# A nucleus search's branch in a graph kernel: two small tie arms for a five-armed switch, its neighbours moved, and the output stores on another queue

## The chip, the cores and the metric

The kernel runs on one core of a Trainium2 chip. The metric is device microseconds of one execution. PE is TensorE, DVE is VectorE, ACT is ScalarE, POOL is GpSimd and SP is SyncE, which here only issues DMAs.

## What is computed

N = 2708 nodes, 512 features. A graph attention layer with 8 heads comes first; its output X goes through two diffusion steps and a layer norm. Cut to what matters:

```python
feats = einsum('nf,hfd->hnd', X, W); dense = leaky_relu(e_self + e_neigh) + mask
X = relu(softmax(dense) @ feats + b)                     # attention over adj
Rf, Rb = S / rowsum(S), S / colsum(S)[:, None]           # S = adj + I
Xf = Xb = Xa = X; Z = 0
for s in range(2):
    logits = (Xa @ W1) @ W2 @ (Xa @ W3).T                # 2708 x 2708
    idx = argsort(-logits)                               # ties: the lower index first
    k_i = sum(cumsum(softmax(sorted logits)) < 0.9) + 1  # the nucleus of each row
    A = softmax(where(rank < k_i, logits, -inf))
    Xf, Xb, Xa = Rf @ Xf, Rb @ Xb, A @ Xa
    Z = Z + Xf @ U1[s] + Xb @ U2[s] + Xa @ U3[s]
out = layernorm(x + Z) * gamma + beta                    # in outline
```

The costly question is the nucleus: for each row, the smallest set of largest probabilities that holds 0.9 of the mass.

## The kernel before

The rows are cut into 22 tiles of 128 (the last has 20) and these into 11 pairs; pair g is tiles 2g and 2g+1. A pair's work in a diffusion step passes through these stages:

- `products`: PE makes a 128 x 2708 tile of logits (L534) and ACT copies it into `p` (L536).
- `exp`: DVE takes the row maxima `nmx` (L561), ACT exponentiates (root and full, L569 to L573) with the row sums.
- `points`: POOL guesses three thresholds for each row from the row sums by a fitted power (L578 to L588): `x` and `pts`, their fourth powers `th`, the negative `nth`, and `thr`, `top`, `cap`.
- the looks: ACT (L566) sums signs of p + nth, and POOL (L591 to L593) makes of that the mass above each guess, in `pts`.
- `Opened`: `ready` (L641 to L643, L655) and `bracket` (L661 to L676), small DVE operations, put those masses into an interval for each row.
- `search`: ROUNDS = (2, 4) rounds in step 0 and 1. Each picks a point in the interval and measures the mass above it in each tile (L647, one pass of a tile).
- `finish`: the entries of the interval are cut out (`kept_from` L773, or `kept_ranked` L778 to L781 in step 1, where equal values are told apart by rank), the largest 8 or 16 are sorted out by MAX8 (L849, L851), and the cut and the denominator `den` follow.
- `branch`: flags of all rows are folded into one integer `code_i`. 0: nothing is left to do. 1, 2, 3: a tile of the pair, or both, has ties at the cut that rank does not settle. 4: a row fell short of its cut. DVE loads it into a register and switches (L936) over five arms. Arm 4 holds more rounds, a second finish with a switch of its own, and in that a third.
- `rden` (L958) is the reciprocal of `den`. `keep`, the pair's kept probabilities, goes to `attended`: PE transposes it (L1107), ACT copies the transposes into `at` (L1111), PE multiplies by Xa (L1127).

The engines' orders in a diffusion step are the order of emission for PE, ACT, DVE and SP (a manual schedule); POOL's order is the scheduler's. The loop over g runs the search of pair g+1 on DVE beside the attended stage of pair g on PE. Between its rounds the search calls `early` (puts `exp` of pair g+2 in: `nmx` on DVE, and a list `fills` for ACT) and what it returns: `norms`, the layer norm's ends of the pair before (L1190, L1191; step 1 only), and `pending`, which splits results for DRAM. In the last two pairs nothing follows to be filled in.

`attended` is a generator. Between its groups n of transposes and products it issues `fills` and `others`. The latter are steps of `part`: the products of S with Xf and Xb (PE L1021, L1024) and with U (L1042), whose operands `hl` and `s_r` are loaded by SP (L1014, L1016) and `u_k` by SP (L1040); then `xe` on ACT and `z` on POOL (L1065, L1067). In step 1 ACT scales the product into `yo` (L1135), POOL adds z (L1137), and `normed` follows: moments (L137 to L140), a load of the input row (`xw`, SP, L1187), the two DVE operations of `rest`, and a store of the finished rows, issued by POOL (L1192).

Step 1 has one piece of work more at its start: `counted` (L1226, DVE), the ranks that settle ties. It comes in two halves, 22 operations in all; the second half stands after the first pair's `nmx` and covers ACT's and POOL's first work on that pair.

The branch as it was:

```python
            opened = None
            if go == 0 and then:
                opened = then()               # Opened(next pair): ready, before the switch
            what = nc.values_load(code_i[0:1, 0:1], engines=[DVE], min_val=0, max_val=1 << G, ...)
            for arm in tc.Switch({DVE: what}, (1 << G) + 1):
                if 0 < arm < 1 << G:
                    ties([x for x in tiles if arm >> x[0] & 1])
                elif arm == 1 << G and go == 0:
                    rounds(MORE_ROUNDS); choose(); finish(1)
                elif arm == 1 << G and go == 1:
                    ...
                    finish(2)
                elif arm == 1 << G:
                    bisect()
                if opened:
                    opened.bracket()
```

Of the kernel before, what the change touches and what calls it, by code (L numbers as in the profile page):

```python
# [15 lines left out]
OP = mybir.AluOpType  # L16
# [17 lines left out]
BISECT_STEPS = 28  # L34
# [11 lines left out]
MORE_ROUNDS = 3  # L46
# [7 lines left out]
def kernel(  # L54
# [428 lines left out]
    for s in range(STEPS):  # L483
        for i in range(2):
            nc.vector.memset(powers[:, s, i], GUESS[s][i])
    about = const.tile([P, STEPS, len(ABOUT), G], F32, name="about")
    for s in range(STEPS):
        for j, m in enumerate(ABOUT):
            nc.vector.memset(about[:, s, j], m * math.exp(GUESS[s][2]))
# [15 lines left out]
    class Logits:  # L505
# [33 lines left out]
        def exp(self, looks=True):  # L539
# [19 lines left out]
            for i, t in enumerate(self.grp):  # L559
                pr = rows[t]  # L560
                nc.vector.tensor_reduce(nmx[:pr, 0, i:i + 1], self.p[i][:pr], axis=AX.X, op=OP.max, negate=True)  # L561

# [13 lines left out]
            def points():  # L576
                x0 = small.tile([P, 2, G], F32, name="x0")
                gp.tensor_tensor(x0, self.sums, powers[:, self.s], op=OP.pow)  # L578
                gp.tensor_tensor(x0[:, 0], x0[:, 0], x0[:, 1], op=OP.mult)
                x = self.pts[:, :, 0]  # L580
                gp.tensor_tensor(x, x0[:, 0].unsqueeze(1).to_broadcast([P, NA, G]), about[:, self.s], op=OP.mult)
                gp.tensor_scalar(x, x, X_LO * 1.2, 0.9995, op0=OP.max, op1=OP.min)
                gp.tensor_tensor(self.th, x, x, op=OP.mult)
                gp.tensor_tensor(self.th, self.th, self.th, op=OP.mult)
                gp.tensor_scalar(self.nth, self.th, -1.0, None, op0=OP.mult)  # L585
                gp.tensor_scalar(self.thr, self.tot, P_NUC, None, op0=OP.mult)
                gp.tensor_scalar(self.top, self.tot, 1.0 + CURVE, None, op0=OP.mult)
                gp.tensor_scalar(self.cap, self.tot, CAP, None, op0=OP.mult)  # L588
# [22 lines left out]
    class Opened:  # L611
# [4 lines left out]
        def __init__(self, lg, looked, junk):  # L616
            _, small, _ = lg.pools
            self.lg, self.looked = lg, looked
# [59 lines left out]
    def search(lg, o, junk, early, late, then=None):  # L678
# [14 lines left out]
        tiles, aim, mass = o.tiles, o.aim, o.mass  # L693
# [7 lines left out]
        def rounds(n, aim_at=None):  # L701
            for it in range(n):
                v.tensor_tensor(d, ends[:, 1, 0:2], ends[:, 0, 0:2], op=OP.subtract)
                v.tensor_scalar(d[:, 1], d[:, 1], -1e-12, None, op0=OP.min)
                v.reciprocal(fr, d[:, 1])
                v.tensor_mul(fr, fr, ends[:, 0, 1])
                v.tensor_scalar(fr, fr, -0.95, -0.05, op0=OP.max, op1=OP.min)
                v.tensor_mul(fr, fr, d[:, 0])
                v.tensor_tensor(cur[:, 0], ends[:, 0, 0], fr, op=OP.subtract)
                v.tensor_mul(th, cur[:, 0], cur[:, 0])  # L710
                v.tensor_mul(th, th, th)
                if it in (aim_at or ()):
                    v.tensor_copy(fr, g0)
                    aim(g0, th)
                    v.tensor_tensor(fr, fr, g0, op=OP.subtract)
                    v.tensor_tensor(ends[:, :, 1], ends[:, :, 1], fr.unsqueeze(1).to_broadcast([P, 2, G]), op=OP.add)
                if begun:
                    begun.pop()()
                for i, pr in tiles:
                    mass(i, pr, th[:pr, i:i + 1], cur[:pr, 2, i:i + 1])  # L720
                v.tensor_tensor(fr, lg.top, cur[:, 2], op=OP.subtract)
                v.reciprocal(fr, fr)
                v.tensor_tensor(cur[:, 1], fr, g0, op=OP.subtract)
                v.scalar_tensor_tensor(side, cur[:, 1].unsqueeze(1).to_broadcast([P, 2, G]), 0.0, sides,
                                       op0=OP.is_ge, op1=OP.not_equal)
                v.copy_predicated(ends, side.unsqueeze(2).to_broadcast([P, 2, 3, G]),
                                  cur.unsqueeze(1).to_broadcast([P, 2, 3, G]))
                if it == s and aim_at is not None:
                    begun.append(early())

        begun = []
        rounds(ROUNDS[s], (0,) if s else ())
        for rest in begun:
            rest()
# [5 lines left out]
        def choose():  # L740


            v.tensor_tensor(low, ends[:, 0, 2], thr, op=OP.is_lt)
            v.tensor_copy(kept[:, 0], ends[:, 1, 0])
            v.tensor_copy(kept[:, 1], ends[:, 1, 2])
            v.copy_predicated(kept[:, 0], low, ends[:, 0, 0])
            v.copy_predicated(kept[:, 1], low, ends[:, 0, 2])
            v.tensor_mul(th, kept[:, 0], kept[:, 0])
            v.tensor_mul(th, th, th)

        choose()
# [32 lines left out]
        def ties(of):  # L784


            if lg.rank is not None:
                for x in of:
                    kept_from(*x)
# [3 lines left out]
            for i, pr in of:  # L793
                v.tensor_scalar(junk_b[:pr], ps_[i][:pr], cut[:pr, i:i + 1], None, op0=OP.is_equal)
# [8 lines left out]
        def bisect():  # L803
# [3 lines left out]
            v.memset(ends[:, 0, 0], X_LO)  # L807
            v.memset(ends[:, 1, 0], X_HI)
            for _ in range(BISECT_STEPS):
                v.tensor_add(cur[:, 0], ends[:, 0, 0], ends[:, 1, 0])  # L810
                v.tensor_scalar(cur[:, 0], cur[:, 0], 0.5, None, op0=OP.mult)
                v.tensor_mul(th, cur[:, 0], cur[:, 0])
                v.tensor_mul(th, th, th)
                for i, pr in tiles:
                    v.scalar_tensor_tensor(junk_b[:pr], ps_[i][:pr], th[:pr, i:i + 1], ps_[i][:pr],
                                           op0=OP.is_ge, op1=OP.mult, accum_out=cur[:pr, 2, i:i + 1])
                v.tensor_tensor(side[:, 0], cur[:, 2], thr, op=OP.is_ge)
                v.tensor_tensor(side[:, 1], cur[:, 2], thr, op=OP.is_lt)
                v.copy_predicated(ends[:, 0, 0], side[:, 0], cur[:, 0])
                v.copy_predicated(ends[:, 1, 0], side[:, 1], cur[:, 0])  # L820
            v.tensor_mul(d, ends[:, :, 0], ends[:, :, 0])
            v.tensor_mul(d, d, d)
            half = junk.shape[1]
            for i, pr in tiles:
                v.scalar_tensor_tensor(keep[i][:pr], ps_[i][:pr], d[:pr, 1, i:i + 1], ps_[i][:pr],
                                       op0=OP.is_ge, op1=OP.mult, accum_out=over[:pr, i:i + 1])
                v.scalar_tensor_tensor(ps_[i][:pr], ps_[i][:pr], d[:pr, 0, i:i + 1], ps_[i][:pr],
# [13 lines left out]
        def finish(go):  # L841
# [16 lines left out]
            if lg.rank is not None:  # L858
# [28 lines left out]
                return branch(go)  # L887
# [25 lines left out]
            branch(go)  # L913

        def branch(go):
# [15 lines left out]
            opened = None  # L931
            if go == 0 and then:
                opened = then()
            what = nc.values_load(code_i[0:1, 0:1], engines=[DVE], min_val=0, max_val=1 << G,
                                  skip_runtime_bounds_check_because="at most 1 << G")
            for arm in tc.Switch({DVE: what}, (1 << G) + 1):  # L936
                if 0 < arm < 1 << G:
                    ties([x for x in tiles if arm >> x[0] & 1])
                elif arm == 1 << G and go == 0:
                    rounds(MORE_ROUNDS)  # L940
                    choose()
                    finish(1)
                elif arm == 1 << G and go == 1:
                    v.copy_predicated(th, short, vn[:, :, nx - 1])
                    v.copy_predicated(kept[:, 1], short, den)
                    finish(2)
                elif arm == 1 << G:
                    bisect()
                if opened:
                    opened.bracket()  # L950
            if go == 0:
                nxt.append(opened)

        nxt = []
        late()
        finish(0)
        rden = small.tile([P, G], F32, name="rden1")
        v.reciprocal(rden, den)  # L958
        return (keep, rden), nxt[0]
# [5 lines left out]
    for s in range(STEPS):  # L965
        last = s == STEPS - 1
        with ExitStack() as st:
# [121 lines left out]
            spread_z = {}  # L1089

# [5 lines left out]
            def attended(grp, keep, rden, fills, others, first=3):  # L1096
# [20 lines left out]
                for n, (i, t, cs) in enumerate(steps):  # L1117
                    pr = rows[t]
                    nxt = turned(*steps[n + 1]) if n + 1 < len(steps) else None
                    if n:  # L1120
                        paced(left, 1)
                    if n >= first:
                        paced(fills, 1 + i if last else 1 if n > 8 else 2)
# [58 lines left out]
            def normed(t, y):  # L1182
# [6 lines left out]
                def rest():  # L1189
                    nc.vector.scalar_tensor_tensor(y[:pr], y[:pr], mean, g_b[:pr], op0=OP.subtract, op1=OP.mult)  # L1190
                    nc.vector.scalar_tensor_tensor(y[:pr], y[:pr], rs, xb[:pr], op0=OP.mult, op1=OP.add)  # L1191
                    nc.gpsimd.dma_start(out=out[cols[t], :], in_=y[:pr])  # L1192
# [53 lines left out]
            with tc.manual_schedule(engines={PE, ACT, DVE, SP}):  # L1246
# [8 lines left out]
                for step in steps:  # L1255
                    step()
# [7 lines left out]
                ready = opened = None  # L1264
                looks, left = [], []
                for g in range(-1, NP):
# [23 lines left out]
                    def early(g=g):  # L1290
                        if g + 2 < NP:
                            fills.extend(lg[g + 2].exp())
                        return lambda: [rest() for rest in norms] + [paced(pending, len(pending))]
# [30 lines left out]
                    if g + 1 < NP:  # L1324
                        if g == 0:
                            opened = Opened(lg[1], True, junk)
                            opened.bracket()
                        then = (lambda g=g: Opened(lg[g + 2], True, junk)) if 0 <= g < NP - 2 else None
                        ready, opened = search(lg[g + 1], opened, junk, early, late, then)
# [5 lines left out]
                if last:  # L1335
                    for rest in [normed(t, y) for t, y in done]:
                        rest()

# [30 lines left out]
```

## Time and profile before

| | us |
|---|---|
| runs | 3674.58, 3666.84, 3673.27 (median 3673.27) |
| profiled execution | 3675.58, span 3673.8 |
| attention layer | to about 1087 |
| diffusion step 0 | about 1087 to 2235 |
| diffusion step 1 | about 2300 to 3668 |
| busy: ACT, POOL | 1499.2 (41%), 867.6 (24%) |

In the profile the idle time of an engine stands with what ended it. "issue" means that the engine waited for nothing that the profile shows. Lines are those of the kernel. The granted clock is that of PE, 1.00 being full speed. Two searches took a tie arm, both in step 1 with one tile each.

### The profile page before, as it was taken

What the parts mean: (1) busy time and instruction counts of PE and PEld (TensorE: products, weight loads), DVE (VectorE), ACT (ScalarE), POOL (GpSimd) and SP (SyncE); (2) the same over time, 40 slices, a digit from 0 to 9 for tenths busy, and PEclk for the clock granted to TensorE, in tenths of its full rate; (3) what the DMA queues carried; (4) which work ended last, traced back from release to release, by engine and by line L of the source; (5) the groups of instructions that cost most, each with busy time, mean ns of one, the idle gap of its engine ahead of it and who ended that gap; (6) DMA issues with size and microseconds to landing.
All of it is one profiled execution on the core that took longest, in us unless ns stands there. A gap on an engine that the chain in (4) does not pass through costs nothing. (4 is left out here: it accounts for less than half of the span.)

```text
span 3673.8 us, 34163 instructions
## 1 busy us (share of the span) xinstructions
PE 3339.6 (91%) x10791; PEld 1725.2 (47%) x10791; DVE 2668.4 (73%) x4832; ACT 1499.2 (41%) x2248; POOL 867.6 (24%) x1072
## 2 busy tenths in 40 slices
PE   8998999998967889999999999978899799999977
PEld 4433333333444454645555454544555455555543
DVE  4587888989965565546563652796889888888984
ACT  2343212011113656666565641235445545456600
POOL 4114241514321021111121111321213232122211
PEclk9999999999979999999999999989999899999989
DMA  4477424232227343526344442782465255654443
GB/s 117 149 250 249 141 76 157 75 106 100 85 80 268 134 165 126 206 87 212 107 162 167 139 168 75 268 282 96 157 215 201 103 181 198 226 198 167 162 133 130
DMA packets 247979, 580.17 MB, mean 158 GB/s; under 512 B 33306, under 2 KB 67050, under 8 KB 243492
## 3 DMA queue, kind: packets, MB, share of 16 engines
q1 hardware_dynamic: 226695, 503.59, 41.0%
q0 software_dynamic: 21040, 73.88, 5.2%
q8 instruction: 86, 1.41, 0.2%
q14 instruction: 158, 1.29, 0.1%
HBM read 471.68 MB, written 105.68 MB: 157 GB/s over the span
## 5 line engine op out<-in xcount | busy, mean ns | idle before, releaser
L1127 PE MATMUL a<-va,at 128*128 128x512 f32 (+2 forms) x1936 | 900.7, 605 | 55.3 <-ACT at L1111 55.1
L442 PE MATMUL po<-e,fw 128*65 128x512 f32 (+4 forms) x2112 | 840.2, 553 | 36.2 <-DVE e L440 20.9
L440 DVE SCALAR_TENSOR_TENSOR e<-r_b,kk,a_c 128x512 f32<-128x512 f32 (+4 forms) x1056 | 751.6, 741 | 74.8 <-PE po L442 25.8
L566 ACT ACTIVATE junk_a<-p,nth 128x2708 uint8<-128x2708 f32 (+1 forms) x240 | 612.7, 2553 | 102.3 <-POOL nth L585 98.1
L1021 PE MATMUL q<-hl,s_r 128*128 128x512 f32 x1936 | 525.2, 420 | 57.5 <-DMA s_r<-s_d 57.3
L1127 PEld LDWEIGHTS a<-va,at 128*128 128x128 f32 (+2 forms) x1936 | 341.6, 189 | 433.6 <-issue 346.1
L442 PEld LDWEIGHTS po<-e,fw 128*65 128x65 f32 (+1 forms) x2112 | 286.7, 140 | 549.4 <-issue 271.9
L1021 PEld LDWEIGHTS q<-hl,s_r 128*128 128x128 f32 x1936 | 362.0, 191 | 208.2 <-issue 58.9
L647 DVE SCALAR_TENSOR_TENSOR junk<-p,th 128x2708 bf16<-128x2708 f32 (+1 forms) x132 | 411.5, 3118 | 3.8
L1042 PE MATMUL q<-u_k,tt 128*128 128x512 f32 x704 | 321.2, 599 | 10.6 <-DMA u_k<-in_L_gnn_U_dram 10.6
L1111 ACT COPY at<-t 128x512 f32<-128x512 f32 (+3 forms) x308 | 140.0, 476 | 466.8 <-PE t L1107 466.1
L1024 PE MATMUL q<-s_r,hl 128*128 128x512 f32 (+1 forms) x1056 | 281.3, 411 | 11.1 <-DMA s_r<-s_d 11.1
L536 ACT COPY p<-t 128x452 f32<-128x452 f32 (+2 forms) x264 | 130.2, 537 | 371.5 <-PE t L534 303.8
L1024 PEld LDWEIGHTS q<-s_r,hl 128*128 128x128 f32 x1056 | 188.1, 189 | 98.2 <-issue 51.3
L534 PE MATMUL t<-keys,q_t 128*128 128x452 f32 x528 | 155.7, 420 | 73.0 <-ACT p L536 59.3
L1042 PEld LDWEIGHTS q<-u_k,tt 128*128 128x128 f32 x704 | 135.6, 193 | 162.7 <-issue 158.6
L851 DVE MAX8 vn<-keep 128x8 f32<-128x2708 f32 (+1 forms) x66 | 196.8, 2981 | 2.3
L424 ACT ACTIVATE s_c<-a_c 128x512 fp32r<-128x512 f32 (+3 forms) x132 | 76.2, 577 | 247.7 <-DMA a_c<-in_adj_t_dram 119.0
L1167 PE MATMUL a<-u_k,v_t 128*128 128x512 f32 (+1 forms) x352 | 173.4, 629 | 0.8 <-DMA u_k<-in_L_gnn_U_dram 0.8
L1107 PEld LDWEIGHTS t<-ident,keep 128*128 128x128 f32 (+1 forms) x968 | 114.6, 140 | 111.1 <-issue 83.8
L561 DVE TENSOR_REDUCE nmx<-p 128x1 f32<-128x2708 f32 (+1 forms) x44 | 129.3, 2966 | 48.8 <-ACT p L536 48.8
L1107 PE MATMUL t<-ident,keep 128*128 128x128 f32 (+1 forms) x968 | 147.5, 275 | 18.6 <-DVE ends L662 10.7
(305 smaller groups left out, 3339.3 us busy)
## 6 DMA issues: line engine op xcount, KB each, us to landing
s_r<-s_d SPq DMA_DIRECT2D x330, 256.0 KB
hl<-vhl_d SPq DMA_DIRECT2D x132, 512.0 KB
hl<-fhl_d SPq DMA_DIRECT2D x132, 512.0 KB
hl<-bhl_d SPq DMA_DIRECT2D x132, 512.0 KB
u_k<-in_L_gnn_U_dram SPq DMA_DIRECT2D x184, 256.0 KB
arow<-in_adj_dram SPq DMA_DIRECT2D x21, 1354.0 KB
s_d<-s_c SPq DMA_DIRECT2D x88, 256.0 KB
a_c<-in_adj_t_dram SPq DMA_DIRECT2D x84, 256.0 KB
```

The costliest lines, as they stand in the source:

```text
L440: nc.vector.scalar_tensor_tensor(e[:pr, :cw], r_b[:pr, i, :cw], kk[:pr, t, hd:hd + 1], a_c[t][:pr, :cw], op0=OP.max, op1=OP.mult)
L442: nc.tensor.matmul(po[i][:, :cw], lhsT=fw[:pr, t, hd, :], rhs=e[:pr, :cw], start=(t == 0), stop=(t == NT - 1))
L534: nc.tensor.matmul(pl[:, :c1 - c0], lhsT=q[:, i], rhs=self.keys[:, c0:c1], start=(i == 0), stop=(i == 1))
L566: nc.scalar.activation(junk[:pr], self.p[i][:pr], func, **kw)
L647: nc.vector.scalar_tensor_tensor(self.junk_b[:pr], p, th, p, op0=OP.is_ge, op1=OP.mult, accum_out=dst)
L851: v.max(vs, keep[0][:pr])
L1021: nc.tensor.matmul(half[j], lhsT=s_r[:, j * P:(j + 1) * P], rhs=hl[:, h], start=(c == 0 and h == 0), stop=(c == NT - 1 and h == 1))
L1024: nc.tensor.matmul(half[j][:, :w], lhsT=hl[:, h, j * P:(j + 1) * P], rhs=s_r[:, :w], start=(c == 0 and h == 0), stop=(c == NT - 1 and h == 1))
L1042: nc.tensor.matmul(half[j], lhsT=across_t[-1][:, k, j * P:(j + 1) * P], rhs=u_k, start=(start and k == 0), stop=(start and k == KD - 1))
L1107: nc.tensor.transpose(pt[:rows[c], j, :pr], keep[i][:pr, cols[c]], ident[:pr, :pr])
L1127: nc.tensor.matmul(pa[:pr], lhsT=at[:rows[c], j, :pr], rhs=va[:rows[c], c, :], start=(c == 0), stop=(c == NT - 1))
L1167: nc.tensor.matmul(pz[i][:rows[t]], lhsT=v_t[i][:, k, :rows[t]], rhs=u_k, start=(k == 0), stop=(k == KD - 1))
```

## The change

- The switch becomes nested conditions: if the code is not 0, then bisection for 4, else one arm for each tile. The arms with more rounds and a second finish are gone, and `bisect` is written anew: 27 geometric steps from 2^-16 in place of 28 arithmetic ones.
- `ready` and `bracket` of the next pair no longer stand before and in the branch, but just before the next search, behind `rden` and the moments of `normed`.
- `points` makes `nth` at once (the fit's powers times four), then `th`, then `pts` by a fourth root (a pow on POOL). `nth` is POOL's 7th operation of the pair instead of the 10th.
- The two maxima `nmx` leave `exp`: the first goes ahead of the second round's masses, behind `pending`, the second behind that round; in step 1's first pair both go behind the second half of `counted`.
- `ties` uses `keep` as it is and does without a second `kept_from`.
- The output stores are issued by SP, in `attended` at n == 4, and the last ones at the end. On SP they stand ahead of the next part's loads of `hl` and `s_r`.

On DVE's program, the stretch that a search with code 0 jumps over was 566 to 681 rows long and is 187 now, in each of the 22 searches.

```diff
-            for arm in tc.Switch({DVE: what}, (1 << G) + 1):
...
+            with tc.If(what != 0):
+                with tc.If(what == 1 << G) as hard:
                     bisect()
-                if opened:
-                    opened.bracket()
+                with hard.Else():
+                    for n, x in enumerate(tiles):
+                        with tc.If(what != (1 << G) - 1 - (1 << n)):
+                            ties([x])
...
-                x = self.pts[:, :, 0]
-                gp.tensor_tensor(x, x0[:, 0].unsqueeze(1).to_broadcast([P, NA, G]), about[:, self.s], op=OP.mult)
-                gp.tensor_scalar(x, x, X_LO * 1.2, 0.9995, op0=OP.max, op1=OP.min)
-                gp.tensor_tensor(self.th, x, x, op=OP.mult)
-                gp.tensor_tensor(self.th, self.th, self.th, op=OP.mult)
-                gp.tensor_scalar(self.nth, self.th, -1.0, None, op0=OP.mult)
+                gp.tensor_tensor(self.nth, x0[:, 0].unsqueeze(1).to_broadcast([P, NA, G]), about[:, self.s], op=OP.mult)
+                gp.tensor_scalar(self.nth, self.nth, -(X_LO * 1.2) ** 4, -0.9995 ** 4, op0=OP.min, op1=OP.max)
+                gp.tensor_scalar(self.th, self.nth, -1.0, None, op0=OP.mult)
+                gp.tensor_tensor(self.pts[:, :, 0], self.th, quarter, op=OP.pow)
...
-            if lg.rank is not None:
-                for x in of:
-                    kept_from(*x)
...
-                v.tensor_scalar(junk_b[:pr], ps_[i][:pr], cut[:pr, i:i + 1], None, op0=OP.is_equal)
+                v.tensor_scalar(junk_b[:pr], keep[i][:pr], cut[:pr, i:i + 1], None, op0=OP.is_equal)
...
+                    if n == 4:
+                        paced(stores, len(stores))
...
-                    nc.gpsimd.dma_start(out=out[cols[t], :], in_=y[:pr])
+                    stores.append(lambda: nc.sync.dma_start(out=out[cols[t], :], in_=y[:pr]))
...
-                for step in steps:
+                for step in lg[0].maxima + steps:
...
                         if g + 2 < NP:
                             fills.extend(lg[g + 2].exp())
-                        return lambda: [rest() for rest in norms] + [paced(pending, len(pending))]
+                        first, *more = lg[g + 2].maxima if g + 2 < NP else [lambda: None]
+
+                        def begin():
+                            paced(pending, len(pending))
+                            first()
+
+                        return begin, lambda: [x() for x in more], lambda: [rest() for rest in norms]
...
-                        if g == 0:
-                            opened = Opened(lg[1], True, junk)
+                        opened = None
+                        if g >= 0:
+                            opened = Opened(lg[g + 1], True, junk)
                             opened.bracket()
-                        then = (lambda g=g: Opened(lg[g + 2], True, junk)) if 0 <= g < NP - 2 else None
-                        ready, opened = search(lg[g + 1], opened, junk, early, late, then)
+                        ready = search(lg[g + 1], opened, junk, early, late)
...
+                    paced(stores, len(stores))
```

## The prediction

> **What bounds the kernel now.** I read the page's busy shares first. TensorE works nine tenths of the span, so a saving on VectorE counts only where TensorE waits for it.
>
> ```profile
> PE 3339.6 (91%) x10791; PEld 1725.2 (47%) x10791; DVE 2668.4 (73%) x4832; ACT 1499.2 (41%) x2248; POOL 867.6 (24%) x1072
> ```
>
> Next I cut the span into stretches (columns: length, then busy time of PE, PEld, DVE, ACT and POOL, granted clock, DMA). The first row is diffusion step 0, the second a quiet pair of step 1, the third the pair after a tie.
>
> ```profile
> 1450.00:1550.00 100.00, 99.76 (x361) 61.52 (x362) 57.92 (x129) 53.90 (x61) 16.36 (x28) 1.00 0.61 210
> 3200.00:3300.00 100.00, 96.08 (x334) 57.72 (x334) 89.42 (x162) 53.55 (x59) 28.57 (x25) 1.00 0.52 179
> 2850.00:2950.00 100.00, 80.06 (x259) 45.07 (x258) 91.97 (x135) 53.53 (x59) 32.46 (x25) 0.90 0.34 118
> ```
>
> Step 0 is TensorE's alone. In step 1 both engines need nearly the whole period (the attended stages start at 2983.0, 3092.9, 3202.4, 3312.5 and 3421.9, so 109.5 to 110 us apart), and TensorE loses time only where VectorE falls behind: the third row. So I looked for VectorE's holes with the table of waits over the whole run (total, times, longest).
>
> ```profile
> DVE pts L655 <- POOL pts L593: 188.5, 11, 33.0
> DVE rden L958 <- issue: 106.4, 22, 6.3
> PE a L1127 <- ACT at L1111: 55.1, 30, 16.7
> ```
>
> The second row is the branch: 22 times VectorE waits for nothing shown, 4.8 us each. The timeline of VectorE around one search without a tie, and then around a tie, shows where.
>
> ```profile
> 2953.75 0.14 DVE L930 TENSOR_SCALAR code_i<-code 1x1 int32<-1x1 f32 x1
> ...
> 2955.58 0.17 DVE L661 TENSOR_SCALAR ends<-sums 128x2 f32<-128x2 f32 x1 [1.07 <-issue]
> ...
> 2962.75 0.17 DVE L958 RECIPROCAL rden<-den 128x2 f32<-128x2 f32 x1 [4.63 <-issue]
> ```
>
> ```profile
> 2823.03 0.14 DVE L930 TENSOR_SCALAR code_i<-code 1x1 int32<-1x1 f32 x1
> ...
> 2828.96 3.04 DVE L773 SCALAR_TENSOR_TENSOR keep<-p,cut 128x2708 f32<-128x2708 f32 x1 [5.17 <-issue]
> ...
> 2854.38 0.17 DVE L958 RECIPROCAL rden<-den 128x2 f32<-128x2 f32 x1 [5.79 <-issue]
> ```
>
> Loading the code and entering arm 0, the next code in line, costs 1.07 us; leaving it over four other arms (566 to 681 rows of the program) costs 4.63, and entering a tie arm, which the switch reaches by a stride of whole padded arms, 5.17. The price goes with the distance. Last, the one large hole of TensorE behind a tie, from the timelines of POOL and ACT.
>
> ```profile
> 2884.04 0.68 POOL L1192 DMA_DIRECT2D out_dram<-yo  x1 [26.87 <-DVE yo L1191]
> 2884.74 1.28 POOL L1067 TENSOR_TENSOR z<-z,xe 128x512 f32<-128x512 f32 x1
> ```
>
> ```profile
> 2886.06 0.69 ACT L1065 ACTIVATE xe<-q,rinv 128x512 f32<-128x512 f32 x1 [19.88 <-POOL z L1067]
> ```
>
> POOL stands 26.87 us before an output store that waits for VectorE's y. `z` is behind it, ACT's `xe` behind `z`, `at` behind `xe`, and TensorE waits 16.7 us for `at`: a queue, not a data dependence.
>
> **The branch.** The jump over the arms shrinks to 187 rows. Bounds from the rows: 1.07 us (entering the next code) and 1.07 + 6.3. I take code to rden at 1.3 us: 187 rows are nearer to the short jump than to 566. Before, it is 8.4 to 10.3 us in step 1's pairs with the opening inside, about 2.5 of them the bracket, which the change puts after rden. Net, about 5 us of VectorE per search, and the keep rows are released at code + 1.3 instead of + 2.3. [...]
>
> **Where that counts.** In step 0 there is one hole behind a branch: at 1341.45 TensorE waits 9.38 us for ACT's p, which waits for the branch, which waited 21.5 us for POOL's pts although its code was ready at 1317.2. With the opening moved behind rden the hole goes: −9.4. VectorE then waits for pts there instead, with nothing of TensorE's behind it; the next search cannot begin before pts in either kernel. The other holes of step 0 (17.88 us behind the first search, some 3 us behind xa) stay. Ten other searches save VectorE time under TensorE's work: 0.
>
> **Ties and hard rows.** No search was ever short or hard: MAX8 (L851) runs 66 times, once for each of 22 tiles in step 0 and twice in step 1, so no second finish; the arms removed and the new bisection cost 0. Two searches tie, one tile each. A second L773 (3.04) goes, entry falls from 5.17 to about 1, exit from 5.79 to about 1: some 12 us of VectorE each.
>
> **Start of step 1.** Before, the two maxima (L561, 5.85) stood between the halves of counted(), and its second half (twelve L1226, 27.65 us) hid ACT's exponentials (11 us) and POOL's points. After, the maxima follow the second half. Then nothing hides them: VectorE ends the maxima at 2361.9, ACT's four activations end at 2370.3, POOL's points, without VectorE beside them, take some 3.3 us as at 2420: first mass at about 2374 instead of 2362.45. Cost +11.4, on the path, since VectorE has no slack up to the first attended stage: it starts at 2501 instead of 2490.0.
>
> **Maxima inside the search.** The first moves ahead of round 1's masses, the second behind round 1. ACT has the first 9 us earlier after rden. In pairs 0 and 1 of step 1, TensorE's holes of 11.34 and 9.25 us are `at` queued on ACT behind nmx; I expect 4 back in pair 0, of which the later pts and a cooler clock eat 2, so 2. In step 0 the first maximum stands behind pending split_hl steps, which wait for a DMA of 4.8 us, and the second behind the masses; slack there is 2 to 7 us: 0, bounds −2 to +6. POOL's shorter chain to nth (7th instead of 10th operation) feeds looks that have slack: 0, and no loss since no operation is longer than the pow of before.
>
> **Stores on SP.** What is queued behind a store that waits for y is now not POOL's z but the next part's loads of hl and s_r. y comes about 35 us after rden (32 to 34.5 before, and the bracket of 2.5); the loads need some 3 us more (a 512 KB transfer lands in 2.9 to 3.9); TensorE needs them 26 us after the attended stage starts. So it waits 12 us less the lead of rden over that start. In quiet pairs the lead is 22 us: 0. In pair 1 it will be near 6.5: 5.5 us, in place of the 9.25 us hole; gain 4, and 1 of clock. After the first tie VectorE comes sooner by 12, and the hole of 16.7 us goes for a wait of 0 to 4: 16.7 less 2, and some 3 for the clock (0.90 in that row), −18. The last pair likewise trades like for like. At the very end the store is issued by SP (0.4 us) instead of POOL (0.55) behind a short chain: −1.5, bounds −3 to 0.
>
> **Sum.** Step 1 in starts of attended stages: 0 at +11, pair 1 at +9, pair 2 at +4 to +5, pair 3 the same, pair 4 at −13, then TensorE-bound to pair 8, the second tie's search ends 10 to 14 earlier, and so the end: −12. With step 0 −9.4 and the store −1.5: −23. From the profiled run (3675.58, span 3673.8 and 1.8 around it) 3652.6; the median of the runs is 2.3 lower: 3650.
>
> **Rivals.** First, the forecast: 3650, chance 0.55. Second, *the branch still costs its 4 to 5 us.* Then step 1 keeps pace with before but pays the start: the gain behind the first tie falls from 18 to some 10, the lead in each pair is 4 us smaller, and of −23 some −3 is left: 3670, chance 0.14. For it speaks that a tie's entry cost 5.17; against it the 1.07 row. Third, on the other side, *the SP queue holds up the loads.* Each attended stage that starts less than 12 us after its rden pays the difference, 5 to 9 us. The stall delays TensorE and not VectorE, so the lead regrows; but if y comes later still or loads land slowly, holds in six pairs at 7 us cost 42 where I counted 5.5 to 10: −23 + 34 is +11, so 3684. It decides from about three holds more than I counted (23/7). Chance 0.2. Against it: leads of 20.2 to 23.3 us in five pairs of before. Fourth, *the start loses nothing* (POOL's points shorter, maxima early in effect) and no hold appears: −23 − 11 − 5, so 3634, chance 0.11.
>
> **How the numbers follow.** Runs of this kernel spread 0.2% (7 us), which is what can be told from no change. Faster by more than that is below 3666: forecast and fourth case, with a part of the second, 0.66. Same, 3666 to 3681: most of the second and a little of the third, 0.15. Slower: most of the third, 0.19. Range 3625 to 3690: from the fourth case with the other bounds that I took at nothing (−1.5 of the store, −2 of split_hl, and 5 of stall behind the maxima that may go too) to the third with the +6 of split_hl.
>
> **What would show it.** Right: rden within 2 us of code_i and its issue row under 30 us in 22 times; no PE hole near 1341; the first mass of step 1 some 11 us after before's; no store on POOL and no 16.7 us hole after the tie; q L1021 waiting for hl or s_r 5 to 6 us in pair 1. Wrong: rden's issue row still near 100 us; q L1021 waiting for DMA in most pairs of step 1; first mass at the old place; step 0 with new waits of p or nmx.

## The result, and the profile after

The changed kernel takes 3670.98 us (median of 12 runs, 3668.72 to 3681.02) beside 3674.27 for the kernel before on the same chips: ratio 0.9994, 95% interval 0.9985 to 1.0004. No difference can be told. I had forecast 23 us less. The profiled execution of the changed kernel is one of its longer ones (3677.04, span 3675.3), so the two traces are compared stage by stage, not by their ends.

The page's shares hardly move, and neither does a quiet stretch of step 1; the stretch after the first tie, 80.06 busy at a clock of 0.90 before, is mended (columns as before).

```profile
PE 3333.6 (91%) x10791; PEld 1728.0 (47%) x10791; DVE 2653.8 (72%) x4829; ACT 1500.3 (41%) x2248; POOL 841.9 (23%) x1028
```

```profile
1275.00:1330.00 55.00, 45.44 (x151) 27.64 (x151) 40.72 (x71) 28.21 (x29) 9.64 (x15) 0.91 0.60 208
1450.00:1550.00 100.00, 98.49 (x354) 59.37 (x353) 61.14 (x139) 59.05 (x70) 21.48 (x29) 1.00 0.62 215
2850.00:2950.00 100.00, 93.69 (x320) 55.55 (x319) 95.83 (x156) 57.40 (x66) 25.48 (x22) 0.98 0.50 170
3200.00:3300.00 100.00, 96.87 (x329) 58.71 (x328) 89.10 (x164) 51.43 (x54) 24.54 (x22) 0.98 0.62 207
```

The first row is new: in step 0's first pair TensorE has 45.44 of 55 us now, at a clock of 0.91. In the kernel before the stretch was full:

```profile
1275.00:1330.00 55.00, 55.00 (x204) 35.05 (x204) 37.69 (x78) 39.08 (x43) 17.00 (x25) 1.00 0.80 277
```

The waits of the whole run (total, times, longest) say what went and what stayed.

```profile
DVE pts L658 <- POOL pts L596: 172.5, 11, 36.7
DVE rden L939 <- DVEq L928: 81.0, 20, 6.7
PE q L1002 <- DMA s_r<-s_d: 72.4, 56, 8.2
ACT junk_a L571 <- POOL nth L586: 51.2, 13, 6.0
PE a L1111 <- ACT at L1093: 15.8, 26, 4.2
```

Two rows of the kernel before stand beside these:

```profile
ACT junk_a L566 <- POOL nth L585: 98.1, 15, 9.3
PE q L1021 <- DMA s_r<-s_d: 57.3, 57, 8.4
```

The branch (second row, now shown as VectorE's own sequencer) is still 4.05 us a time, after 4.84. TensorE waits 39 us less for `at`, and 15 us more for `s_r`: the queue behind a store moved from POOL to SP. ACT waits 47 us less for POOL's `nth`.

How far TensorE is behind the kernel before, by the starts of its attended stages:

| stage | before | after | difference |
|---|---|---|---|
| step 0, first | 1230.1 | 1232.7 | +2.6 |
| step 0, second | 1349.2 | 1362.0 | +12.8 |
| step 0, ninth | 2079.9 | 2091.5 | +11.6 |
| step 1, first | 2490.0 | 2512.2 | +22.2 |
| step 1, second | 2614.7 | 2639.3 | +24.6 |
| step 1, fifth (after the first tie) | 2983.0 | 2980.0 | −3.0 |
| step 1, ninth | 3421.9 | 3418.8 | −3.1 |
| step 1, tenth (after the second tie) | 3521.6 | 3521.9 | +0.3 |

So 2.6 us were lost by the first stage of step 0 and 10.2 in the pair behind it, 11 at the start of step 1, and 28 came back up to the fifth stage of step 1. The loss in the pair is a chain over three engines, from the timelines of DVE, ACT and PE.

```profile
1282.66 0.43 DVE L181 TENSOR_SCALAR split_hl<-xe 128x512 int32<-128x512 int32 x1 [2.17 <-DMA bhl_d<-split_hl]
...
1283.73 2.97 DVE L564 TENSOR_REDUCE nmx<-p 128x1 f32<-128x2708 f32 x1
```

```profile
1286.73 0.20 ACT L574 ACTIVATE nmx<-nmx 128x1 f32<-128x1 f32 x1 [13.21 <-DVE nmx L564]
...
1292.19 0.56 ACT L149 COPY v_t<-t 128x512 f32<-128x512 f32 x1
```

```profile
1292.81 1.12 PE L1089 MATMUL t<-ident,keep 128*128 128x128 f32 x4 [8.51 <-ACT v_t L149]
```

The maximum stands behind `pending`, whose split_hl operations wait for a DMA; it comes at 1283.73 instead of 1270.35. ACT holds its queue for it for 13.21 us, `v_t` and `at` are behind, and TensorE stands 8.51 us.

The second loss is the start of step 1: 45.1 us from the end of counted's first half (2336.8) to the first mass, where there were 34.1 (2328.35 to 2362.45), so +11.0. The first mass before, and after:

```profile
2362.45 3.04 DVE L647 SCALAR_TENSOR_TENSOR junk<-p,th_a 128x2708 bf16<-128x2708 f32 x1 [0.68 <-POOL th_a L584]
```

```profile
2381.89 3.04 DVE L650 SCALAR_TENSOR_TENSOR junk<-p,th_a 128x2708 bf16<-128x2708 f32 x1 [11.35 <-POOL th_a L587]
```

### The profile page after: what moved, and what is told of

Its sections match the earlier page's. It is cut to its first block, busy times and chain, and to the rows that moved or that the text cites. A ratio compares the mean times of both kernels' runs of the same rounds, so it can differ in the third digit from the quotient of the medians.

```text
span 3675.3 us, 33992 instructions
## 1 busy us (share of the span) xinstructions
PE 3333.6 (91%) x10791; PEld 1728.0 (47%) x10791; DVE 2653.8 (72%) x4829; ACT 1500.3 (41%) x2248; POOL 841.9 (23%) x1028
## 5 line engine op out<-in xcount | busy, mean ns | idle before, releaser
L440 DVE SCALAR_TENSOR_TENSOR e<-r_b,kk,a_c 128x512 f32<-128x512 f32 (+4 forms) x1056 | 749.7, 739 | 73.4 <-PE po L442 23.7
L571 ACT ACTIVATE junk_a<-p,nth 128x2708 uint8<-128x2708 f32 (+1 forms) x240 | 612.7, 2553 | 55.5 <-POOL nth L586 51.2
L650 DVE SCALAR_TENSOR_TENSOR junk<-p,th 128x2708 bf16<-128x2708 f32 (+1 forms) x132 | 423.1, 3205 | 3.3
```

The lines of the kernel that those rows point to most:

```text
L440: nc.vector.scalar_tensor_tensor(e[:pr, :cw], r_b[:pr, i, :cw], kk[:pr, t, hd:hd + 1], a_c[t][:pr, :cw], op0=OP.max, op1=OP.mult)
L571: nc.scalar.activation(junk[:pr], self.p[i][:pr], func, **kw)
L650: nc.vector.scalar_tensor_tensor(self.junk_b[:pr], p, th, p, op0=OP.is_ge, op1=OP.mult, accum_out=dst)
```

## The experiments

All ratios are to the kernel before, run beside each kernel; times are medians. The medians of the kernel before lay between 3673.0 and 3676.0 us there, so a difference between the medians of two experiments is uncertain by 2 or 3 us. E1 to E5 and E8 are the changed kernel with one edit.

**E1: the first maximum ahead of split_hl.**

```diff
-                            paced(pending, len(pending))
                             first()
+                            paced(pending, len(pending))
```

> Only edit: the first maximum of the next pair goes ahead of the pending split_hl steps instead of behind them. Theory A (in step 0's first pair the maximum waits behind four split_hl operations and two DMA waits, ACT waits 13.2 us for it, and TensorE 8.5 us for ACT's v_t, at a clock of 0.91): the 8.51 us hole of TensorE near 1293 goes, the second attended stage of step 0 starts near 1352 instead of 1362.0, and since step 0 is TensorE's, the whole run is 9 to 11 us shorter, near 3660. Rival (that lateness comes from the first branch's later release, and the looks behind it): the second attended stage still starts after 1358, time within 3 us of the changed kernel.

Measured 3678.6 us, ratio 1.0013 (1.0002 to 1.0023), and the second attended stage starts at 1361.38, 130.0 us after the first (129.3 in the changed kernel). The start of that stage was the rival's (after 1358), the time neither's, and the rival's reason was not shown: ACT's row for the second maximum, now the one behind split_hl and two masses, reads

```profile
1294.79 0.20 ACT L574 ACTIVATE nmx<-nmx 128x1 f32<-128x1 f32 x1 [11.88 <-DVE nmx L564]
```

and TensorE's hole came back at 1300.87 with 12.06 us. The two maxima are one wait: whichever is late holds ACT. The run was 8 us longer than the changed kernel, though its first 2500 us are not slower. In the trace the 8 us come between the fourth and the fifth stage of step 1 (121.4 us instead of 113.5), behind the first tie: its entry cost 4.39 us instead of 1.50, and TensorE then waited 6.84 us for `s_r` instead of 2.94. Why the entry was dearer, with nothing edited there, is not settled.

**E2: the first pair's maxima ahead of counted's second half.**

```diff
+                for step in lg[0].maxima:
+                    step()
                 if last:
                     counted()
-                for step in lg[0].maxima + steps:
+                for step in steps:
```

> Only edit: in step 1's first pair both maxima stand before the second half of counted again, as in the kernel before. Theory A (the cover of ACT's exponentials and POOL's points was lost): the first mass of step 1 starts right after counted, near 2371 instead of 2381.9, the first attended stage of step 1 near 2502 instead of 2512, and the run is 7 to 11 us shorter. Rival B (later pairs have room and swallow it): the start is early, but the last attended stage starts within 3 us of that of the changed kernel, time the same.

Measured 3663.1, ratio 0.9973 (0.996 to 0.9985), 8 us below the changed kernel.

```profile
2364.20 3.02 DVE L1210 SCALAR_TENSOR_TENSOR junk<-keep,own 20x2708 bf16<-20x2708 f32 x1
...
2367.64 3.04 DVE L650 SCALAR_TENSOR_TENSOR junk<-p,th_a 128x2708 bf16<-128x2708 f32 x1 [0.41 <-POOL th_a L587]
```

The first mass follows counted at once, 14.3 us earlier than after; the first attended stage starts at 2498.97 and the ninth at 3406.89, still 12 earlier. Theory A holds.

**E3: a jump of 25 rows.**

```diff
-                with tc.If(what == 1 << G) as hard:
-                    bisect()
-                with hard.Else():
-                    for n, x in enumerate(tiles):
+                for n, x in enumerate(tiles):
```

> The bisection for hard rows is left out (no row needs it here), so that a search with code 0 jumps over some 25 rows instead of 187. [...] Rival C (any taken branch of VectorE costs 3 to 6 us, however short): code_i to rden stays at 3.5 us and more, time the same within 3 us.

Measured 3647.7, ratio 0.9926 (0.9908 to 0.9944): 23 us below the changed kernel. In the table of waits:

```profile
DVE rden L936 <- DVEq L928: 16.6, 20, 1.1
```

All 20 searches without a tie now cost 0.74 to 1.10 us, where 19 of them cost 3.33 to 6.72 in the changed kernel. Nothing but the length of what is jumped over was changed (and with it, the place of all the code that follows): over 25 rows the jump is cheap, and rival C is out. The two traces also say where the dear jumps were paid. E3's stages start 5.5 us earlier than the changed kernel's at the first stage of step 0 (2.5 of them from ahead of the first branch), still only 6.4 at the ninth, 9.4 at the first of step 1, 12.5 at its ninth and 18.8 at its tenth, behind the second tie. Under TensorE's work in step 0 the branch was worth next to nothing, as the prediction had it.

**E4: the stores on POOL.**

```diff
-                    stores.append(lambda: nc.sync.dma_start(out=out[cols[t], :], in_=y[:pr]))
+                    nc.gpsimd.dma_start(out=out[cols[t], :], in_=y[:pr])
```

> Only edit: the output stores are issued by POOL again, right behind rest. Theory A (the store on POOL holds z, the store on SP holds hl and s_r): the waits of q for s_r of 6.9, 2.9 and 6.4 us in the pairs after 2640, 2890 and 3550 go, a hole of 10 us or more for at near 2890 comes back; net 0 to 8 us longer than the changed kernel. Rival D (the SP queue is what ate the gain): the time falls by 6 us or more.

Measured 3672.6, ratio 0.9995 (0.9985 to 1.0004). The waits of 6.89, 2.94 and 6.38 us for `s_r` went, and a hole for `at` of 6.29 us came at 2892, not of 10 or more. The two queues weigh the same here.

**E5: both maxima ahead of split_hl and of the second round's masses.**

```diff
                         def begin():
-                            paced(pending, len(pending))
                             first()
+                            for x in more:
+                                x()
+                            paced(pending, len(pending))
 
-                        return begin, lambda: [x() for x in more], lambda: [rest() for rest in norms]
+                        return begin, lambda: None, lambda: [rest() for rest in norms]
```

> Both maxima of the next pair stand ahead of the pending split_hl steps and of the second round's masses, in both steps. Theory A2 (in step 0's first pair whichever maximum stands behind split_hl and the masses holds ACT; the run with the first alone ahead had its hole of 12.06 us behind the second): TensorE's hole near 1293 or 1300 goes, the second attended stage of step 0 starts near 1350, 129.3 us after the first becomes 118 to 120, and the run is 8 to 13 us shorter than the changed kernel, near 3660. Rival (ACT is late in that pair for its looks, not for the maxima): the distance of the two stages stays above 125 us and the time within 3 us.

Measured 3666.5, ratio 0.9974 (0.9963 to 0.9984). The hole is gone, and the second attended stage starts 116.5 us after the first. That is 12.8 us less than after and 2.6 less than before (119.2): the theory holds for the place. Of the 12.8 the median shows 4.5 (7 by the ratios), below what was expected; the profiled execution (span 3659.6) shows all of it. After the first tie, whose entry cost 3.81 us there, that run has a wait for `s_r` of 6.93 us where the changed kernel had 2.94: the pattern of E1.

**E6 and E7: all three, with the stores on SP and on POOL.** E6 joins the diffs of E2, E3 and E5; E7 adds that of E4.

> Together: both maxima ahead of split_hl, those of step 1's first pair ahead of counted's second half, and the short jump (the bisection for hard rows is left out; no row needs it here); stores from SP. If the three losses lie in different places and add: 3671 less 10, 8 and 23 is 3630, or 3626 to 3640. If they cover each other: no faster than the short jump alone, 3648.

> As the run with all three and stores from SP, but the output stores from POOL. The stores themselves were worth nothing in the changed kernel (3672.6 against 3671.0). With VectorE earlier, y comes earlier and neither queue holds long: within 4 us of that run. Rival (with all else gone the queue decides): more than 6 us apart.

E6: 3631.7, ratio 0.9877 (0.9857 to 0.9897). The three losses add: singly they were 8, 4.5 and 23. E7: 3621.5, ratio 0.9853 (0.983 to 0.9876), the best of all. It is 10 us below E6, the rival's number: with the other holes gone, the queue of the stores counts. There are only four runs of each, and they just touch (3624.8 to 3634.0, and 3613.2 to 3625.4), so the size is rough; the traces agree with it. TensorE waits 86.7 us for `s_r` (both rows together) in E6 and 67.8 in E7, and 7.27, 3.01 and 7.48 us of E6's stand at 2637, 2862 and 3518, each in a pair whose stores were held.

**E8: a jump of 117 rows.**

```diff
-BISECT_STEPS = 27
+BISECT_STEPS = 13
```

> Bisection of 13 steps in place of 27 (too few for a hard row; none is here): the jump is some 117 rows long instead of 187 (which cost 3.3 to 6.7 us in 19 of 20) or 25 (0.74 to 1.10 in 20 of 20). [...] Rival Q (a distance between 117 and 187 decides, or between 25 and 117): all of them alike.

There is one run of this kernel (3656.8 us). In it 15 of the 20 cost 1.07 to 1.38 us, 5 cost 3.29 to 4.97 (the one of 3.29 is put down to ACT in the trace). Rival Q was not right: they are not all alike. With 25, 117 and 187 rows, 0, 5 and 19 of 20 are dear (3.29 us or more). What decides for the single jump is not shown.

**E9: the changed kernel complete, with the order of E5, E2 and E4.** The bisection is in, and the jump is 187 rows.

> The changed kernel, complete with its bisection (jump of 187 rows), with both maxima ahead of split_hl, those of step 1's first pair ahead of counted's second half, and the stores from POOL. Against the same with the short jump (3621) only the jumps' 3 to 5 us are back: if they are worth what they were in the changed kernel (23 us), 3644; range 3636 to 3655. If the losses cover each other, 3660 or more.

Measured 3655.0, ratio 0.9945 (0.9932 to 0.9959). That is the far edge of the expected range. It is the best version that also treats hard rows, 16 us below the changed kernel. Against E7 the long jumps cost 33 us, more than E3's 23.

**E10: E7 with POOL's points in the old order.**

> As the run with all three and stores from POOL (3621), with POOL's points in the old order: nth is POOL's 10th operation again and the fourth root goes. Theory A (the looks have room): within 4 us of 3621. Rival (the earlier looks free ACT, and TensorE behind it): 6 us or more longer.

Measured 3638.4, ratio 0.9897 (0.9882 to 0.9912): 17 us longer than E7, the rival's. ACT waits 102.2 us for `nth` instead of 73.4, TensorE 27.5 for `at` instead of 20.7, with a hole of 5.61 us after the first tie that E7 has not. By the starts of the stages, 5.4 of the 17 us are lost between the ninth and the tenth stage of step 0 (88.9 us instead of 83.5), and 7.3 between the fourth and the fifth of step 1, behind that tie.

**B1 and B2: the kernel before with the short branch, and with the new points besides.**

```diff
-            for arm in tc.Switch({DVE: what}, (1 << G) + 1):
...
+            with tc.If(what != 0):
+                for n, x in enumerate(tiles):
+                    with tc.If(what != (1 << G) - 1 - (1 << n)):
+                        ties([x])
+            if opened:
+                opened.bracket()
```

> The kernel before with nothing changed but its branch: the switch becomes two conditions with one tie arm each (more rounds and bisection for hard rows are left out; no row needs them here), and the bracket of the next pair follows behind it. Theory A (the change's good is the branch, and what came with it cost as much): this alone gives most of the run with all three mended and stores from POOL (3621), that is 3620 to 3635. Rival (moving the opening, the points and the ties' pass are worth as much as the branch): 3640 or more.

> The kernel before with the two short conditions (3646 alone; hard rows left out) and POOL's points in the new order, nothing else. Theory A3 (the earlier nth is worth time by itself: taking it back cost 17 us in the run with everything mended): 3625 to 3636. Rival (it counts only beside the other mends, or that difference was in the jitter): within 5 us of 3646.

B1: 3646.1, ratio 0.992 (0.9907 to 0.9934), the rival's range: the branch alone is worth 30 us against the kernel before beside it (3676.0) and is not the whole of E7. B2: 3634.5, ratio 0.9892 (0.9876 to 0.9909): the points are worth 11.6 us by themselves (10 by the ratios), as E10 had it from the other side. In the traces 4.4 of them are again between the ninth and the tenth stage of step 0 (88.5 us in B1, 84.1 in B2). From B2 to E7 some 13 us are left for the opening, the ties' pass and the order of the maxima in step 1, which were not parted.

## Why the prediction was wrong

It was −23 and the measured median is −3, within the noise. Four terms of the sum were mis-sized; two of the errors were losses that I had priced too low, one a gain too high, one a gain at nothing.

**The first maximum: taken at 0, bounds −2 to +6.** It cost 12.8 us by E5 (129.3 against 116.5). I had seen that split_hl waits for a DMA and that ACT's slack is 2 to 7 us, but set the 4.8 us wait against it alone. The maximum came 13.4 us later: 2.7 from the first branch, 1.7 from the second round's small operations, which now stand ahead of it too, and 8.9 from the split, its operations and its two waits (4.50) together. The trace of before had it: ACT already waited 2.50 us there.

```profile
1273.35 0.20 ACT L569 ACTIVATE nmx<-nmx 128x1 f32<-128x1 f32 x1 [2.50 <-DVE nmx L561]
```

**The hole of 9.38 us: taken as −9.4.** It became 6.32, so 3.06 went. The wait had two causes in a row: ACT was at the looks until 1337.9, and only the last 2.94 us before its copy were the branch's. The table names the last releaser of the engine that waits (ACT's p), and I put the whole of it down to what ended last. PE and ACT before, then after, where ACT copies right behind its last look:

```profile
1341.45 4.98 PE L534 MATMUL t<-keys,q_t 128*128 128x452 f32 x12 [9.38 <-ACT p L536]
1337.73 0.19 ACT L566 ACTIVATION_READ_ACCUMULATOR junk_a<-p,nth 128x1 f32 x1
1340.86 0.97 ACT L536 COPY p<-t 128x452 f32<-128x452 f32 x2 [2.94 <-DVE ends L662]
```

```profile
1353.18 0.19 ACT L571 ACTIVATION_READ_ACCUMULATOR junk_a<-p,nth 128x1 f32 x1
1353.27 0.95 ACT L538 COPY p<-t 128x452 f32<-128x452 f32 x2
1353.84 6.46 PE L536 MATMUL t<-keys,q_t 128*128 128x452 f32 x15 [6.32 <-ACT p L538]
```

The experiments settle it. With the opening behind rden the hole is 6.32 us whether the jump is short (E3, E6, E7) or long (E1, E5, E9); with the opening ahead of a short branch it is 8.95 (B1) and 8.94 (B2).

These two make 19 us, nearly all of the error of 20: at the ninth stage of step 0 the traces have +11.6 where −9.4 was forecast.

**The branch: taken at 1.3 us from code to rden.** The wait in rden's row was 3.3 to 6.7 in 19 of 20 and 1.10 once:

```profile
3391.52 0.14 DVE L925 TENSOR_SCALAR code_i<-code 1x1 int32<-1x1 f32 x1
3392.76 0.17 DVE L939 RECIPROCAL rden<-den 128x2 f32<-128x2 f32 x1 [1.10 <-DVEq L928]
```

No run shows 1.3 us as the price of 187 rows: code to rden was 1.24 once, and the wait alone was 3.33 us or more in the other 19. My reason from the rows, that 187 is nearer to the short jump than to 566, was an estimate with no row between them. E3 (25 rows, 0.74 to 1.10 us in all 20) and E8 (117 rows, 3.29 or more in 5 of 20) are those rows. The release of ACT behind the branch went wrong with it: I had it at code + 1.3 instead of + 2.3. At the first search the kernel before let ACT go at its arm's entry, 1.8 us after the code began (1220.17), and the changed one only behind the jump, 4.0 us after (1220.24), which is nearly all of the +2.6 of the table's first row.

```profile
1221.97 0.97 ACT L536 COPY p<-t 128x452 f32<-128x452 f32 x2 [12.13 <-DVEq L936]
```

```profile
1224.28 0.97 ACT L538 COPY p<-t 128x452 f32<-128x452 f32 x2 [14.53 <-DVEq L928]
```

**The points: taken at 0.** "Looks that have slack" was wrong: they were worth 11.6 us (B2) to 17 us (E10). The looks stand on ACT ahead of `at` and `p`, so ACT's wait for `nth` (98.1 us before, 51.2 after) was partly TensorE's.

The last two errors point opposite ways, the branch a loss of 23 to 33 us and the points a gain of 11.6 to 17, each measured in other kernels than the changed one. That they offset each other in step 1 would be why its stages look well forecast: fifth stage against step 0's end −14.6 (forecast −13). This was not parted stage by stage, and I cannot claim it as the sum's merit.

**What was right.** The start of step 1: +11.4 forecast, +11.0 in the trace, and E2 shows it. The 3.3 us taken for POOL's points without VectorE beside them held: up to `th_a` they took 3.1. One of their operations, beside `counted` in E2 and beside an idle VectorE in the changed kernel, shows the difference:

```profile
2358.32 2.83 POOL L584 TENSOR_TENSOR x<-x 128x2 f32<-128x2 f32 x1
```

```profile
2380.78 0.19 POOL L584 TENSOR_TENSOR x<-x 128x2 f32<-128x2 f32 x1
```

The stores: 5.5 us in pair 1 and 0 to 4 after the tie, measured 6.89 and 2.94, and 6.38 in the last pair, and TensorE's hole of 16.7 us behind POOL's store went.

```profile
2672.86 3.75 PE L1002 MATMUL q<-hl,s_r 128*128 128x512 f32 x8 [6.89 <-DMA s_r<-s_d]
```

The ties: the pass of 3.04 us went, and the first tie's code to rden fell from 31.35 to 15.77 us. The second gave only 6.5 of its 12, because its entry, taken at 1, cost 6.97 us (under 1 in E3, with the short jump):

```profile
3507.61 0.16 DVE L793 TENSOR_TENSOR over<-den,thr 128x2 f32<-128x2 f32 x1 [6.97 <-issue]
```

The second rival's 3670 is the measured time, and its price of the jump was right (4.05 us a time), but it still counted the 9.4 of step 0, no loss by the maximum and no gain by the points: right by offset. The third rival, the SP queue, did not decide in this kernel (E4); once the rest is mended it is worth some 10 us (E6 against E7).

## What to carry to other kernels

Before moving an operation behind others, add up everything on its engine up to its new place, waits included, and compare that with the slack of the engine that reads it; when two like operations feed one queue, move both. Of a wait in the profile, look at what the releasing engine did just before: only the part that it spent idle goes with the cause. Here the jump over rare code cost more where that code was longer (0.74 to 1.10 us over 25 rows in E3, 3.33 to 6.72 over 187 in 19 of 20 searches of the changed kernel), so keep rare code short, and measure a length between the two you know before you take a price from the nearer one.

## What the runs showed of the hardware

VectorE's jump over code that a search does not need cost 0.74 to 1.10 us over 25 rows (E3, 20 of 20 searches), 1.07 to 1.38 (15 of 20) or 3.29 to 4.97 (5 of 20) over 117 (E8), and 3.33 to 6.72 over 187 in 19 of the 20 searches without a tie of the changed kernel. The remaining one, the twentieth of the 22 searches, had a cheap jump of 1.10 us; what made it cheap is not shown. Behind it VectorE stood 2.86 us after rden with nothing shown to wait for, so that jump and wait together took 3.96 us. Over the whole kernel the price is 23 us (E3 against the changed kernel) to 33 us (E7 against E9).

A small operation of POOL (128 x 2, float32) took 2.83 us while VectorE worked through `counted`, and 0.19 us while VectorE stood idle (E2 and the changed kernel).
